# A macaron layer on one core: weight loads moved to GpSimd's queue, the bias added by a DMA

## The chip, the core and the metric

The kernel runs on one core of one Trainium2 chip. The metric is the device time of one launch in microseconds; the number to compare is the median of several runs.

## What is computed

The layer takes x of shape 2 x 1024 x 1024 in float32 and applies three residual steps: half a feed-forward step, attention, and the same half feed-forward step again, each behind a layernorm without weights:

```
x = x + 0.5 * ffn(layernorm(x))
x = x + attn(layernorm(x))
x = x + 0.5 * ffn(layernorm(x))

ffn(x)  = x @ base_w.T + base_b + 2.0 * sum over the top 2 of 8 experts of
          weight_e * (x @ lora_A[e].T) @ lora_B[e].T      # rank 16, gate: softmax of the top 2 of x @ gate_w.T
attn(x) = causal attention, 32 query heads, 8 key/value heads, width 32, rotary positions, then @ Wo
```

The bias base_b has 1024 entries. It is added with a factor of one half in both feed-forward steps.

## The kernel before

The 2048 rows of x are cut into 16 tiles of 128 rows. A tile goes through four stages, which the code calls a1 (first feed-forward step), a2 (products with Wq, Wk, Wv), c1 (product with Wo) and c2 (second feed-forward step); attention runs between a2 and c1 in units of one tile and one key/value head. In the order of instructions, dense stages of some tiles are cut into pieces and placed between the attention units of another.

Every float32 product is made from float16 parts: an operand is scaled and split into a high and a low half, and `dense` (L353 to L362) multiplies high by high, high by low and low by high (L358, L359, L360). So the beginning of the kernel has a preparation for each weight: it is loaded in float32, the sum of squares is taken (`pow2`, L165 to L188, with squares on ScalarE at L169, a small product on TensorE at L174 and a root on GpSimd at L177), and `split` (L190 to L195) writes the high half on ScalarE (L194) or, for every fourth block, on GpSimd (L192), and the low half on VectorE (L195). Base, gate and lora weights stay in SBUF (`wb`, `ag`, `lbh`, `lbl`). The five halves of Wq, Wk with Wv, and Wo are written back to HBM in their split form (`wstr`, L267) and streamed in for each tile by `prefetch` (L366 to L371) into three half buffers `ws` that are used in turn.

`layernorm` (L328 to L351) takes statistics on VectorE (L331, L333), a root on GpSimd (L335, L337), the normalised tile `xn` on ScalarE (L349), and has `Split.add` write its high (L310, ScalarE) and low half (L311, VectorE) to `hl`. A DMA transposition on SP's queue (L314) turns `hl` into `tt`, the left operand. `ffn` (L390 to L447) first multiplies `tt` with the gate and lora_A weights, then adds the bias `bb` to the tile with two GpSimd additions of 128 x 512 (L395), computes the expert weights (L398 to L420), makes the two base products (n = 0 and 1, L358 to L360, with the lora part at L440 to L442), and adds each to the tile on VectorE (L444).

Loads are issued by `load_x` (L124 to L127) for a tile of x and by `piece` (L143 to L163) for half a weight column block, 1 MB, in up to two DMAs; `stage` (L245) is `piece` for one of the streamed weights. Each takes the engine that issues the DMA. In the kernel before this is SP, except for Wk and Wv, which ScalarE's queue issues (L794, L795). `bb` is loaded by one DMA that repeats the bias on 128 partitions (L793), and is halved on ScalarE (L233, `prep_lora`). The beginning is written out in order at L770 to L831: loads, then a1 of tiles 0 to 2 in pieces, with the preparation between them.

The order of instructions on each engine is set by a scheduler that simulates a timeline, so an edit can move instructions that it doesn't name. `pin` (L117 to L120) keeps the DMAs of the beginning in the order of the program. A queue's DMAs are issued in order: one that waits holds up those behind it, and on GpSimd, whose DMAs stand in one order with its arithmetic, the arithmetic too.

Of the kernel before, what the change touches and what calls it, by code (L numbers as in the profile page):

```python
# [9 lines left out]
FP = mybir.dt.float32  # L10
# [3 lines left out]
ALU = mybir.AluOpType  # L14
AX = mybir.AxisListType

B, T, D = 2, 1024, 1024
NH, NKV, DH, GRP = 32, 8, 32, 4
E, R = 8, 16
P = 128  # L20
KB = D // P
# [18 lines left out]
def kernel(  # L40
# [16 lines left out]
    nc = tc.nc  # L57
# [3 lines left out]
    const = ctx.enter_context(tc.tile_pool(name="const", bufs=1))  # L61
    wres = ctx.enter_context(tc.tile_pool(name="wres", bufs=1))
    small = ctx.enter_context(tc.tile_pool(name="small", bufs=SB))
# [4 lines left out]
    dram = ctx.enter_context(tc.tile_pool(name="dram", bufs=1, space=bass.MemoryType.DRAM))  # L68
# [17 lines left out]
        out=cmask, in_=cmask, compare_op=ALU.is_ge, fill=-NEG, base=0,  # L86
# [14 lines left out]
    nc.gpsimd.memset(ones, 1.0)  # L101
    cosT = const.tile([P, TPB, DH // 2], FP)
    sinT = const.tile([P, TPB, DH], FP)
    bb = const.tile([P, D], FP)

    qst = [stat.tile([P, NH, P], HP, name=f"qst{j}") for j in range(2)]
    kst = stat.tile([P, NKV, P], HP)
# [9 lines left out]
    def pin(ins):  # L117

        if pinned[0]:
            tc.keep_in_program_order(ins)  # L120
# [3 lines left out]
    def load_x(t):  # L124
        xt = xp.tile([P, D], FP, name="xt")
        pin(nc.sync.dma_start(out=xt, in_=late["x"] if t == LATE and late else xf[bass.ts(t, P), :]))
        xts[t] = xt  # L127
# [15 lines left out]
    def piece(slot, srcs, h, eng):  # L143

        if slot < 0:
            st = wss[slot].rearrange("p a k n -> p (a k n)").bitcast(FP)
            st = st.rearrange("p (k n) -> p k n", n=512)
        elif slot >= 3:
            st = (qst + [kts[:, HK : 2 * HK]])[slot - 3]
            st = st.rearrange("p k h c -> p (k h c)" if slot == 5 else "p h c -> p (h c)")  # L150
            st = st.bitcast(FP).rearrange("p (k n) -> p k n", n=512)
        else:
            st = stg.tile([P, HK, 512], FP, name=f"st{slot}")
        c = 0
        for src in srcs:
            n = src.shape[1]
            ins = eng.dma_start(
                out=st[:, :, c : c + n],
                in_=src[h * (D // 2) : (h + 1) * (D // 2), :].rearrange("(k p) n -> p k n", p=P),
            )  # L160
            pin(ins)
            c += n
        return st  # L163
# [61 lines left out]
    def prep_lora(st):  # L225
        c = const.tile([P, 2], FP, name="sl")
        nc.vector.tensor_copy(c[:, 0:1], S["l",])
        nc.vector.scalar_tensor_tensor(c[:, 1:2], INV["b", 0], S["l",], S["b", 1], ALU.mult, ALU.mult)
        for n in range(2):
            h, s = bass.ts(n, 512), c[:, n : n + 1]  # L230
            nc.scalar.activation(lbh[:, h], st[:, h], AF.Copy, scale=s)
            nc.vector.scalar_tensor_tensor(lbl[:, h], st[:, h], s, lbh[:, h], ALU.mult, ALU.subtract)
        nc.scalar.mul(bb, bb, 0.5)  # L233

    KV = [wk_in, wv_in]
    CHUNKS = {
# [8 lines left out]
    def stage(ci, h, slot, eng):  # L245
        staged[ci, h] = piece(slot, CHUNKS[ci][0], h, eng)
# [4 lines left out]
    def prep_stream(ci, slots, after, keep):  # L251

        parts = CHUNKS[ci][1]
        sts = [staged.pop((ci, h)) for h in range(2)]
        sps = []
        for h in range(2):
            sps.append(wss[slots[h]] if slots[h] < 3 else kth)
            if h == 0:
                for name, c0, c1 in parts:
                    pow2([st[:, :, c0:c1] for st in sts], [sps[0][:, j, :, c0:c1] for j in range(2)], name)  # L260
                    yield
            sp = sps[h]
            for k in range(HK):
                for name, c0, c1 in parts:
                    split(sp[:, 0, k, c0:c1], sp[:, 1, k, c0:c1], sts[h][:, k, c0:c1], S[name], k)
                yield
            nc.scalar.dma_start(out=wstr[ci, h], in_=sp)  # L267
            if keep:
                stream.append((ci, sp))
            if after[h]:  # L270
                stage(*after[h], nc.sync)
            yield True

    def prep_rest():
# [115 lines left out]
    def ffn(xt, tt, done):  # L390
        psa = p_dense.tile([P, 512], FP, name="pd")
        yield from dense(psa[:, 0 : P + E], tt, lambda k: (ag[:, 0, k, :], ag[:, 1, k, :]))
        for n in range(2):
            c = bass.ts(n, 512)
            nc.gpsimd.tensor_tensor(xt[:, c], xt[:, c], bb[:, c], ALU.add)  # L395

        lg = small.tile([P, E], FP, name="lg")
        nc.scalar.activation(lg, psa[:, P : P + E], AF.Copy, scale=S["cg"])  # L398
        nv = small.tile([P, 1], FP, name="nv")
        nc.vector.tensor_reduce(nv, lg, AX.X, ALU.max, negate=True)  # L400
        ex = small.tile([P, E], FP, name="ex")
        nc.scalar.activation(ex, lg, AF.Exp, bias=nv)
        fe = lg.unsqueeze(1).to_broadcast([P, E, E])
        ee = lg.unsqueeze(2).to_broadcast([P, E, E])
        lw = small.tile([P, E, R], FP, name="lw", bufs=1)
        gt, eq = lw[:, :, 0:E], lw[:, :, E : 2 * E]
        nc.vector.tensor_tensor(gt, fe, ee, ALU.is_gt)
        nc.vector.tensor_tensor(eq, fe, ee, ALU.is_equal)
        nc.vector.tensor_tensor(eq, eq, tri, ALU.mult)
        nc.vector.tensor_tensor(gt, gt, eq, ALU.add)  # L410
        rk = small.tile([P, E], FP, name="rk")
        nc.vector.tensor_reduce(rk, gt, AX.X, ALU.add)
        nc.vector.scalar_tensor_tensor(ex, rk, 1.5, ex, ALU.is_lt, ALU.mult)
        sm = small.tile([P, 1], FP, name="sm")
        nc.vector.tensor_reduce(sm, ex, AX.X, ALU.add)
        nc.vector.reciprocal(sm, sm)
        nc.vector.tensor_scalar(ex, ex, sm, S["inva2"], ALU.mult, ALU.mult)
        nc.vector.tensor_tensor(
            lw, psa[:, 0:P].rearrange("p (e r) -> p e r", r=R),
            ex.unsqueeze(2).to_broadcast([P, E, R]), ALU.mult,  # L420
        )
        yield True
        psb = [None, None]
        lh = ll = None
        for n in range(2):
            ps = p_dense.tile([P, 512], FP, name="pd")
            psb[n] = ps
            yield from dense(
                ps, tt, lambda k: (wb[:, n, 0, k, :], wb[:, n, 1, k, :]), last=False
            )  # L430
            if n == 0:
                pst = p_s1.tile([P, GRP, P], FP, name="s1")[:, 0, :]
                nc.tensor.transpose(pst, lw.rearrange("p e r -> p (e r)"), ident)
                lh = small.tile([P, P], HP, name="lh", bufs=LB)
                ll = small.tile([P, P], HP, name="ll", bufs=LB)
                nc.scalar.copy(lh, pst)
                nc.vector.tensor_tensor(ll, pst, lh, ALU.subtract)
                yield
            c = bass.ts(n, 512)
            nc.tensor.matmul(ps, lhsT=lh, rhs=lbh[:, c], start=False, stop=False)  # L440
            nc.tensor.matmul(ps, lhsT=lh, rhs=lbl[:, c], start=False, stop=False)
            nc.tensor.matmul(ps, lhsT=ll, rhs=lbh[:, c], start=False, stop=True)  # L442
            yield
            nc.vector.scalar_tensor_tensor(xt[:, c], ps, S["uf", n], xt[:, c], ALU.mult, ALU.add)  # L444
            done(n)
            if n == 0:
                yield True  # L447

    def stage_a1(t):
        tt = layernorm(xts[t])  # L450
        yield

        def done(n):
            if n == 1:
                Ts["x2", t] = layernorm(xts[t])
                if t == LATE:
                    late["x"] = dram.tile([P, D], FP, name="xlate")
                    nc.sync.dma_start(out=late["x"], in_=xts.pop(t))

        yield from ffn(xts[t], tt, done)  # L460
        yield True
# [318 lines left out]
    gst = [agst[:, h] for h in range(2)]  # L780
    lst = xp.tile([P, D], FP, name="xt")
    pin(nc.sync.dma_start(out=lst, in_=lb_in))
    b0 = [piece(h - 2, [wb_in[:, 0:512]], h, nc.sync) for h in range(2)]
    load_x(1)
    a1 = [stage_a1(t) for t in range(3)]
    next(a1[0])
    prep_gate(gst)
    pow2([lst[:, bass.ts(h, 512)] for h in range(2)], [lbh[:, bass.ts(h, 512)] for h in range(2)], ("l",))
    b1 = [piece(3 + h, [wb_in[:, 512:1024]], h, nc.sync) for h in range(2)]
    prep_base(0, b0)  # L790
    load_x(2)
    next(a1[1])
    pin(nc.sync.dma_start(out=bb, in_=bias_in.partition_broadcast(P)))  # L793
    stage(2, 0, 0, nc.scalar)  # L794
    stage(2, 1, 1, nc.scalar)  # L795
    prep_base(1, b1)
    prep_lora(lst)
    stage(3, 0, 2, nc.sync)
    stage(3, 1, 5, nc.sync)
    stage(0, 0, 3, nc.sync)  # L800
    stage(0, 1, 4, nc.sync)
    next(a1[2])
    pin(nc.sync.dma_start(out=cosT, in_=cos_in.rearrange("(i p) d -> p i d", p=P)))
    pin(nc.sync.dma_start(out=sinT, in_=sin_in.rearrange("(i p) d -> p i d", p=P)))
# [235 lines left out]
```

## Time and profile before

| what | us |
|---|---|
| median of 3 runs | 1523.7 |
| lowest and highest | 1520.88, 1530.89 |
| profiled execution | 1528.72 |
| its span on the core | 1527.0 |
| TensorE busy in the span | 1404.1 |
| GpSimd busy in the span | 450.1 |
| GpSimd's bias additions (L395), 64 of them | 92.3 |

The profile is one execution, recorded by the hardware. PE is TensorE's matmul, PEld its weight load, DVE is VectorE, ACT ScalarE, POOL GpSimd, SP SyncE; SPq, ACTq and POOLq are the instruction queues of these engines where they issue DMAs. A line such as L395 is a line of the kernel before. Start times count from the start of the span. "Idle before, releaser" says how long an engine stood still ahead of an instruction and what ended it. DMA issues do not count as busy time of an engine. The granted clock is the share of full speed that TensorE was given.

### The profile page before, as it was taken

The page shows a single profiled execution, that of the slowest core. Times are in us where ns is not written, and L with a number is a line of the kernel's source. Part 1 is how long each engine was busy: PE and PEld are TensorE (multiplying, and loading weights), DVE is VectorE, ACT ScalarE, POOL GpSimd, SP SyncE. Part 2 cuts the span into 40 slices and gives each one's busy share as a digit, 9 for nine tenths or more (in the row PEclk, how much of TensorE's full clock was granted, in tenths as well). Part 3 has the DMA queues.
Part 4 walks back from the last instruction along what each step waited for, and adds up shares of the span by engine and source line. Part 5 has one row for each costly group of instructions (what it writes and reads, how often), then busy time and mean ns, then how long its engine had stood idle before and what let it go on. Part 6 is the DMA issues. An engine that isn't in the chain of part 4 may idle for free.

```text
span 1527.0 us, 35303 instructions
## 1 busy us (share of the span) xinstructions
PE 1404.1 (92%) x14548; PEld 783.4 (51%) x14548; DVE 1139.7 (75%) x2420; ACT 755.5 (49%) x1374; POOL 450.1 (29%) x665
## 2 busy tenths in 40 slices
PE   3686897989999999999999899999999999989998
PEld 2243444455555555555654445555555555556544
DVE  6877656686968879789764767886869788689753
ACT  7564334453545545456552434553545455556631
POOL 3443213432323233122121323332323232312231
PEclk9798999989999999999999999999999999999999
DMA  9957697658575581853646769857383853834651
GB/s 274 333 156 204 115 237 205 206 127 264 123 238 137 153 254 31 235 160 69 209 160 191 216 161 272 202 160 234 72 294 69 237 147 70 271 69 98 133 170 45
DMA packets 293075, 267.30 MB, mean 175 GB/s; under 512 B 258480, under 2 KB 261552, under 8 KB 272432
## 3 DMA queue, kind: packets, MB, share of 16 engines
q1 hardware_dynamic: 289360, 252.45, 60.5%
q10 hardware_dynamic: 3552, 12.58, 2.3%
q8 instruction: 114, 1.87, 0.5%
q14 instruction: 49, 0.40, 0.1%
HBM read 181.63 MB, written 20.45 MB: 132 GB/s over the span
## 4 chain that ended last, share of the span: by engine, by line
PE 65%; DVE 13%; DMA 13%; ACT 3%; issue 2%; POOL 1%; SPq 1%; DVEq 0%; ACTq 0%; POOLq 0%
PE pd L358 13%; PE pd L359 13%; PE pd L360 13%; PE av L657 10%; PE s L712 7%; PE s L573 6%; DMA ws<-wstr 6%; DMA qt<-qst 5%; DVE mx L590 3%; DVE pair L636 1%; DVE ws L195 1%; DMA tt<-hl 1%; DVE o L666 1%; ACT p L718 1%; DVE hl L311 1%
## 5 line engine op out<-in xcount | busy, mean ns | idle before, releaser
L718 ACT ACTIVATE p<-s,cs 128x512 f32<-128x512 f32 x576 | 382.3, 688 | 291.2 <-PE s L712 284.1
L590 DVE TENSOR_REDUCE mx<-s 128x4 f32<-128x512 f32 x480 | 313.6, 675 | 68.3 <-PE s L573 46.8
L358 PE MATMUL pd<-ws,tt 128*128 128x512 f16 x592 | 226.8, 383 | 20.9 <-DMA ws<-wstr 16.8
L636 DVE TENSOR_TENSOR pair<-p,p 128x512 f32<-128x512 f32 x256 | 185.6, 727 | 72.6 <-ACT p L718 34.8
L573 PE MATMUL s<-kts,qt 96*128 96x128 f16 x2304 | 217.0, 222 | 23.8 <-DMA qt<-qst 17.8
L359 PE MATMUL pd<-ws,tt 128*128 128x512 f16 x592 | 226.3, 382 | 0.0
L712 PE MATMUL s<-qt,kts 128*128 128x512 f16 x576 | 210.7, 386 | 16.4 <-DMA qt<-qst 11.6
L360 PE MATMUL pd<-ws,tt 128*128 128x512 f16 x592 | 225.4, 382 | 0.0
L573 PEld LDWEIGHTS <-qt 96*128 96x128 f16 x2304 | 165.5, 99 | 116.4 <-issue 30.4
L359 PEld LDWEIGHTS <-tt 128*128 128x128 f16 x1360 | 135.6, 100 | 141.9 <-issue 31.3
L358 PEld LDWEIGHTS <-tt 128*128 128x128 f16 x1360 | 135.6, 100 | 135.5 <-issue 16.7
L358 PE MATMUL pd<-wb,tt 128*128 128x512 f16 x512 | 199.0, 389 | 5.0 <-DVE xt L444 5.0
L360 PEld LDWEIGHTS <-tt 128*128 128x128 f16 x1360 | 135.3, 99 | 131.5 <-issue 10.2
L359 PE MATMUL pd<-wb,tt 128*128 128x512 f16 x512 | 198.0, 387 | 0.5 <-DVE wb L195 0.5
L360 PE MATMUL pd<-wb,tt 128*128 128x512 f16 x512 | 197.7, 386 | 0.0
L657 PE MATMUL av<-p,va 128*32 128x128 f32 x4608 | 166.8, 278 | 4.8 <-ACT o L664 2.5
L720 POOL TENSOR_SCALAR_AFFINE_SELECT p<-p 128x512 f32<-128x512 f32 x128 | 89.0, 698 | 274.7 <-ACT p L718 264.4
L673 POOL TENSOR_TENSOR tt<-o,tt 128x128 f16<-128x128 f32 x128 | 70.5, 551 | 279.6 <-ACT tt L672 279.3
L657 PEld LDWEIGHTS av<-p,va 128*32 128x32 f32 x4608 | 115.5, 110 | 68.3 <-issue 53.4
L666 DVE RECIPROCAL o<-o 128x128 f32<-128x128 f32 x128 | 120.6, 942 | 24.9 <-ACT o L664 24.9
L585 POOL TENSOR_SCALAR_AFFINE_SELECT sm<-sm 128x512 f32<-128x512 f32 x96 | 66.4, 692 | 203.9 <-ACT sm L584 202.1
L395 POOL TENSOR_TENSOR xt<-xt,bb 128x512 f32<-128x512 f32 x64 | 92.3, 1464 | 59.6 <-ACT xn L349 59.4
(177 smaller groups left out, 1808.2 us busy)
## 6 DMA issues: line engine op xcount, KB each, us to landing
ws<-wstr SPq DMA_DIRECT2D x148, 1024.0 KB, 5.9
wstr<-ws ACTq DMA_DIRECT2D x9, 1024.0 KB, 6.1
xt<-in_x_dram SPq DMA_DIRECT2D x16, 512.0 KB, 3.8
out_dram<-xt SPq DMA_DIRECT2D x15, 512.0 KB, 2.8
ws<-in_wb_dram SPq DMA_DIRECT2D x2, 1024.0 KB, 8.0
qst<-in_wb_dram SPq DMA_DIRECT2D x2, 1024.0 KB, 6.8
st<-in_wo_dram SPq DMA_DIRECT2D x2, 1024.0 KB, 10.0
kts<-in_wo_dram SPq DMA_DIRECT2D x2, 1024.0 KB, 12.0
```

Source lines behind the costliest of these rows:

```text
L358: nc.tensor.matmul(ps, lhsT=th, rhs=wh, start=(k == 0), stop=False)
L359: nc.tensor.matmul(ps, lhsT=th, rhs=wl, start=False, stop=False)
L360: nc.tensor.matmul(ps, lhsT=tl, rhs=wh, start=False, stop=(last and k == KB - 1))
L395: nc.gpsimd.tensor_tensor(xt[:, c], xt[:, c], bb[:, c], ALU.add)
L573: nc.tensor.matmul(ps[:, h, :], lhsT=q[0 : 3 * DH, h, :], rhs=KT[b0 + j][0 : 3 * DH, g, :], start=(not pem or h == 0), stop=not pem,)
L590: nc.vector.tensor_reduce(mx[:, odd, j, :], ps, AX.X, ALU.max)
L636: nc.vector.tensor_tensor(sums, us[i][1], us[i + 1][1], ALU.add)
L657: prev = nc.tensor.matmul(av[rows, i, :], lhsT=w, rhs=p32[:, h, :], start=(us[0][0] == 0 and n == 0), stop=(last and n == len(runs) - 1), ...
L666: nc.vector.reciprocal(rc, rc)
L712: ins = nc.tensor.matmul(ps.rearrange("p h k -> p (h k)"), lhsT=KT[b0 + j][:, g, :], rhs=q.rearrange("p h k -> p (h k)"), start=True, stop ...
L718: nc.scalar.activation(p32, ps, AF.Exp, scale=cs)
L720: nc.gpsimd.affine_select(out=p32, in_=p32, compare_op=ALU.is_ge, fill=0.0, base=0, pattern=[[0, GRP], [1, P]], channel_multiplier=-1,)
```

## The change

All float32 weight loads of the base, Wq, Wk, Wv and Wo move to GpSimd's queue; x, the gate and lora weights, the rotary tables and the transpositions stay on SP's. The bias is no longer kept on 128 partitions. It is loaded once as 128 x 8, halved on GpSimd, and stored to a 4 KB tensor `hb` in HBM. In each `ffn`, one DMA from GpSimd's queue reads `hb` for all 128 partitions and adds it to the tile of x in SBUF, in place of the two additions. The buffer `bb`, its load and its scaling on ScalarE are gone. The new small load and store stand behind the load of tile 1.

```diff
-    bb = const.tile([P, D], FP)
...
-        nc.scalar.mul(bb, bb, 0.5)
...
             if after[h]:
-                stage(*after[h], nc.sync)
+                stage(*after[h], nc.gpsimd)
...
-        for n in range(2):
-            c = bass.ts(n, 512)
-            nc.gpsimd.tensor_tensor(xt[:, c], xt[:, c], bb[:, c], ALU.add)
+        nc.gpsimd.dma_start(out=xt, in_=hb.partition_broadcast(P), accum_op=ALU.add)
...
-    b0 = [piece(h - 2, [wb_in[:, 0:512]], h, nc.sync) for h in range(2)]
+    b0 = [piece(h - 2, [wb_in[:, 0:512]], h, nc.gpsimd) for h in range(2)]
     load_x(1)
+    hs = small.tile([P, KB], FP, name="hs", bufs=1)
+    pin(nc.sync.dma_start(out=hs, in_=bias_in.rearrange("(p k) -> p k", k=KB)))
+    nc.gpsimd.tensor_scalar(hs, hs, 0.5, 0.0, ALU.mult, ALU.add)
+    hb = dram.tile([D], FP, name="hb")
+    nc.gpsimd.dma_start(out=hb.rearrange("(p k) -> p k", k=KB), in_=hs)
     a1 = [stage_a1(t) for t in range(3)]
...
-    b1 = [piece(3 + h, [wb_in[:, 512:1024]], h, nc.sync) for h in range(2)]
+    b1 = [piece(3 + h, [wb_in[:, 512:1024]], h, nc.gpsimd) for h in range(2)]
     prep_base(0, b0)
     load_x(2)
     next(a1[1])
-    pin(nc.sync.dma_start(out=bb, in_=bias_in.partition_broadcast(P)))
-    stage(2, 0, 0, nc.scalar)
-    stage(2, 1, 1, nc.scalar)
+    stage(2, 0, 0, nc.gpsimd)
+    stage(2, 1, 1, nc.gpsimd)
     prep_base(1, b1)
     prep_lora(lst)
-    stage(3, 0, 2, nc.sync)
-    stage(3, 1, 5, nc.sync)
-    stage(0, 0, 3, nc.sync)
-    stage(0, 1, 4, nc.sync)
+    stage(3, 0, 2, nc.gpsimd)
+    stage(3, 1, 5, nc.gpsimd)
+    stage(0, 0, 3, nc.gpsimd)
+    stage(0, 1, 4, nc.gpsimd)
```

## The prediction

> **What bounds the kernel now.** I read the page's busy shares first, then busy time by stage, then the chain and single rows where the change works.
>
> ```profile
> PE 1404.1 (92%) x14548; PEld 783.4 (51%) x14548; DVE 1139.7 (75%) x2420; ACT 755.5 (49%) x1374; POOL 450.1 (29%) x665
> ...
> L395 POOL TENSOR_TENSOR xt<-xt,bb 128x512 f32<-128x512 f32 x64 | 92.3, 1464 | 59.6 <-ACT xn L349 59.4
> ```
>
> TensorE is busy 92% of 1527.0 us, so 122.9 us of idle is all that a better order can win. GpSimd, whose adds (L395, 92.3 us) go away, is idle 71% of the time: its busy time as such is worth nothing. Busy time by stage (length, then busy time of PE, PEld, DVE, ACT, POOL, granted clock, DMA share, GB/s) shows where the idle lies:
>
> ```profile
> 0.00:60.00 60.00, 24.85 (x114) 13.79 (x114) 45.80 (x128) 42.74 (x69) 25.93 (x51) 0.85 0.95 276
> 60.00:160.00 100.00, 81.52 (x386) 37.96 (x387) 68.01 (x156) 47.94 (x73) 32.07 (x44) 0.90 0.75 222
> ...
> 600.00:700.00 100.00, 98.59 (x1241) 58.91 (x1240) 82.12 (x166) 57.24 (x101) 28.68 (x38) 1.00 0.58 161
> ...
> 900.00:1000.00 100.00, 94.48 (x947) 52.79 (x947) 76.80 (x171) 49.90 (x95) 36.42 (x57) 1.00 0.78 198
> ```
>
> The first 60 us hold 35.2 us of PE's idle, the next 100 us 18.5. From 160 us on, 1297.7 of 1367 us are busy: the remaining 69 us are scattered. So there are two questions: what the start gains, and what 32 new accumulating DMAs cost the full stages. The chain in the start (start, length, what):
>
> ```profile
> 19.70 9.36 DMA xt<-in_x_dram
> 29.07 0.69 DVE bst L331
> 29.77 1.12 DVE hl L311
> 30.92 5.57 DMA tt<-hl
> 36.54 0.30 PE pd L358
> ```
>
> Tile 2's x is issued at 19.70, behind two 1 MB pieces of the base weights on SP's queue, and takes 9.36 us where the median of all x loads is 3.5. VectorE waits for it in order, with tile 1's low half (L311) queued behind it, so tile 1's transposition starts at 30.92 and PE has its first product of tile 1 at 36.54.
>
> **The change, part by part.** The built order of the changed kernel gives what stands behind what on each queue.
>
> *Weights off SP's queue.* SP loses 12 loads, ACT 4; GpSimd gets these 16, one tiny scaling, one 4 KB store and 32 accumulates. Tile 2's x then has no weights ahead of it on its own queue. The Trainium skill, DMA: Bandwidth & Descriptors, section Issuing engines are not separate DMA queues, speaks against a gain: all queues share 16 DMA engines, and only issue time is saved. Read strictly, the 2.5 MB of this moment stay one lump: 9.36 us, gain 0. But its section Queues, rings and completion order has the engines go round between queues packet by packet; then the 0.5 MB need only about 1 MB moved, some 4 us, and the load ends near 24. The row (9.36 beside 3.5) can't choose between the two. It matters little: in the new DVE order tile 1's L311 stands ahead of tile 2's statistics, so tile 1 no longer waits for that load. I estimate its transposition at 26 to 27, so PE gets tile 1 at about 32: minus 4.5 us at this step.
>
> *Issuing on GpSimd.* No DMA is issued from GpSimd before. Bounds per issue: SP's plain loads take 0.43 us each at the start; the longest plain issue on ACT's queue is 2.64 us (wv, with a stall in it). The same page, Specifications, gives about 1 us to the first byte by software descriptors against 0.6 by hardware; this trace has only the hardware kind. I take 1.0 us. In the new order: after L187 (ends 14.56) come two base pieces, scaling, the 4 KB store; then L335 and L337 for tile 1 (before: 18.12 to 19.55); then four K/V pieces, and only then L177 of base half 0 (before: 20.09). At 1.0 us the first three end at 17.8 and hide under the wait for tile 1's statistics; the four K/V issues do not, so L177 comes at 23.6: plus 3.5 us. Next, two accumulates wait for the 4 KB store, which queues behind 2 MB on the same queue: about 25. After them stand GpSimd's own splits of base half 0 (L192, before: 21.57), now at about 28. VectorE's products (L195, before: done at 28.11) end near 30, so tile 0's first dense block ends near 32, not 30.0. But PE idled from 30.0 to 36.5 there, so this is covered as long as tile 1's products come at 36.5 or earlier; net of the first part, PE is then 2 to 4 us ahead. I count minus 3. Later issues (two wo, two wq pieces ahead of the K and V scales; two wq and two wo ahead of tile 0's second layernorm) are eight, and half of their 8 us, 4 us, is on the path: VectorE is full from 40 to 60 us, which hides the others. Without that cover it is 8.
>
> *The bias.* Removed: bb's 512 KB load (4.9 us to landing), L233 on ACT (1.05 us), 64 adds. In the start six adds run from 44.11 and collide with VectorE:
>
> ```profile
> 44.11 8.37 POOL L395 TENSOR_TENSOR xt<-xt,bb 128x512 f32<-128x512 f32 x6
> ```
> ```profile
> 31.47 0.21 DVE L407 TENSOR_TENSOR lw<-lg 128x64 f32<-128x64 f32 x1
> ...
> 46.46 1.21 DVE L407 TENSOR_TENSOR lw<-lg 128x64 f32<-128x64 f32 x1
> 47.59 1.30 DVE L408 TENSOR_TENSOR lw<-lg 128x64 f32<-128x64 f32 x1
> 48.81 0.74 DVE L444 SCALAR_TENSOR_TENSOR xt<-pd,uf,xt 128x512 f32<-128x512 f32 x1
> ```
> ```profile
> 44.24 0.61 PE L442 MATMUL pd<-lbh,ll 128*128 128x512 f16 x1 [1.69 <-DVE ll L437]
> 49.60 0.59 PE L358 MATMUL pd<-wb,tt 128*128 128x512 f16 x1 [4.76 <-DVE xt L444]
> ```
>
> The same tiny L407 takes 0.21 us alone and 1.21 beside the adds. Excess there: L311 0.9, L407 1.0, L408 1.1, L409 0.4, L410 0.5, together 3.9 us in a stage where VectorE is full. PE waits 4.76 us for L444. Without adds L444 can follow L442 at about 45; of the 4.76 us I count 3, since four other VectorE instructions stand in between, part of the 3.9 us. Together minus 5. In the full stages an add costs PE next to nothing: waits of PE on VectorE's mx and pair are 5.7 and 2.7 us over the whole run. I count minus 1.
>
> *32 accumulates.* Is each in time for L444? In the full stage xn of a tile ends at 659.5, L444 runs at 679.9: 20 us of cover; for the last tile 1501.9 to 1521.9. The nearest row, bb's load of the same shape, lands in 4.9 us; a queue full of weights may double it. So the wait is covered. What is not covered is the load on the engines. A plain 512 KB at the best 10 us window (410 GB/s) is 1.3 us of all 16 engines. By the skill's DMA page (Rules for kernel authors) an accumulate reads its destination too and writes it later: source, destination, write, 1.5 MB, 3.8 us as an estimate. Such DMAs are not in the trace; I take 2.6. 27 of them fall after 160 us, 70 us of DMA work, 5% on shares of 0.53 to 0.78. PE's waits for DMAs there:
>
> ```profile
> PE pd L358 <- DMA ws<-wstr: 16.8, 15, 2.2
> PE s L712 <- DMA qt<-qst: 11.6, 12, 2.1
> PE s L573 <- DMA qt<-qst: 9.3, 8, 2.4
> ```
>
> With tt's 3 these are 38 waits out of some 320 transfers, 12%. If each accumulate holds up one or two transfers by 2.6 us and 12% of these are waited for, it is 8 to 17 us; some of it lies in slack between the transfers, so I take 9. Ends: 0 (all slip into free slots) and 27 x 3.8 = 103 (every one on the path; excluded by the 12%), realistically 40.
>
> **Sum.** Against the profiled execution (1528.7 us, span 1527.0): start minus 3 plus 4 minus 5 is minus 4; full stages plus 9 minus 1. Plus 4. That execution lay 5 us above the median of 1523.7, so I put the same plus 4 on the median, 1528, and one more microsecond for the changed order in the stage from 60 to 160 us, whose waits for transpositions I can't place: 1529.
>
> **Rivals.**
>
> *Slower: accumulates hold up the streamed weights and q's transpositions.* One mechanism, in the stages with DMA shares over 0.7 (160 to 400, 800 to 1000 us). Three half buffers of weights are used in turn, so a load that lands late moves the next one. For: those 38 waits are short (2.4 us at most), so loads land close to their use and PE has little left over. Against: from 400 to 800 us PE is 97 to 99% busy at shares near 0.57. Price: 27 x 2.6 us x 0.35 on the path is 25 us, with the start's minus 4 and minus 1 1544; at 3.8 us each 1556. I give 1548. It decides, that is, passes 15 us, from about 0.27 of each delay on the path.
>
> *Slower: GpSimd's issue takes 2.6 us, not 1.* Then L177 of base half 0 comes at about 33.5 instead of 20.1, tile 0's first dense block ends 13 us later, of which 6.5 us of idle absorb half: plus 6.5; eight later issues at half: plus 10; minus 5 for the bias; plus 8 full stages: 1543. It decides from about 2 us an issue.
>
> *Faster: the start gains in full.* Tile 1's 4.5, PE's 4.8 before L444, 3.9 of collisions, and 18 matmuls that now run at half clock (0.43 us instead of 0.22) behind the waits of 49.6 and 61.2 us, 3.8: minus 17, with accumulates free: 1507. Against: VectorE is full from 40 to 60 us and bounds what the start can gain.
>
> **How the numbers follow.** Likeliest 0.40 (1529, own range 1513 to 1540); accumulates 0.30 (1548; nine in ten over 1%); issue 0.14 (1543; seven in ten over 1%); faster 0.16 (1507; some eight in ten over 1%). About 1%, 15 us, is what a measurement here tells from no change. Slower: 0.27 + 0.10 = 0.37, rounded up to 0.39 for the upper end of the likeliest; faster 0.13; same 0.48. The range leaves out half of the fast case and the end of the accumulates: 1508 to 1562.
>
> **What would show it.** Right: tile 1's tt starts near 27; the 4.76 us wait before L358 is gone and L407 takes 0.2 us throughout; no wait of L444 on a DMA; GpSimd's gaps of about 1 us per issue; PE's waits on ws and qt up from 37.7 us by 5 to 15. Wrong: L177 of base half 0 after 28 us (issue dearer), L444 waiting for the accumulate (cover gone), or PE's waits on ws and qt doubled.

## The result and the profile after

The changed kernel takes 1538.56 us (median of 7 runs, 1533.11 to 1549.86) against 1521.27 us before (7 runs, 1516.24 to 1530.89): ratio 1.0117, 95% interval 1.0089 to 1.0144. It is slower by 1.2%. Some executions, of e4, e5 and e8 below, run in a slower state at a lower granted clock; the ratios leave these out, the medians in us don't. The profiled execution took 1538.56 us with a span of 1536.9; that of before had a span of 1527.0. The granted clock over the whole span is 0.974 in both.

In the changed kernel lines up to L391 are one or two lower than before, later ones four: the first product of `dense` is L356 (L358 before), the transposition L312 (L314), the tile update L440 (L444), the accumulating DMA L391.

The page of the kernel after, its busy shares, the costliest VectorE group of attention, and the accumulating DMA (issues, KB each, median us to landing):

```profile
PE 1397.8 (91%) x14548; PEld 782.1 (51%) x14548; DVE 1111.7 (72%) x2420; ACT 753.4 (49%) x1373; POOL 397.8 (26%) x651
...
L632 DVE TENSOR_TENSOR pair<-p,p 128x512 f32<-128x512 f32 x256 | 177.1, 694 | 72.7 <-ACT p L714 30.7
...
xt<-hb POOLq DMA_DIRECT2D x32, 512.0 KB, 6.6
```

GpSimd and VectorE have less work, as the edit promised, and the kernel is slower all the same. Busy time by stage of the kernel after (columns as in the prediction) tells where to look:

```profile
0.00:60.00 60.00, 16.50 (x92) 10.75 (x93) 31.36 (x105) 35.06 (x53) 29.74 (x60) 0.97 0.90 232
60.00:160.00 100.00, 77.25 (x369) 36.45 (x366) 69.33 (x166) 54.59 (x88) 32.35 (x49) 0.90 0.77 228
600.00:700.00 100.00, 98.85 (x1187) 58.42 (x1186) 81.06 (x168) 52.95 (x96) 24.01 (x36) 1.00 0.63 167
```

PE has 16.50 us of work in the first 60 us where it had 24.85, and 77.25 in the next 100 where it had 81.52. From 600 to 700 us it is as busy as before (98.85 and 98.59). The times at which a tile's output is issued need no window, and they are used for every run below (the last tile goes out in two pieces; the table has the first):

| output of tile | before, us | after, us | lag |
|---|---|---|---|
| first | 276.42 | 282.28 | 5.9 |
| second | 346.51 | 360.48 | 14.0 |
| third | 428.95 | 442.96 | 14.0 |
| sixth | 726.02 | 744.07 | 18.1 |
| ninth | 1016.65 | 1034.42 | 17.8 |
| last | 1522.69 | 1532.38 | 9.7 |

The lag is 5.9 us at the first output, 14.0 at the second, grows by 4 us more, and shrinks towards the end. What is lost is lost early: before the first output and between the first and the second. PE's waits in the first 160 us (total, number, longest), first before, then after:

```profile
PE pd L358 <- DVE xt L444: 5.0, 2, 4.8
PE pd L358 <- DMA tt<-hl: 1.8, 2, 1.5
```
```profile
PE pd L356 <- DMA tt<-hl: 25.2, 2, 15.1
```

The 5.0 us of waiting for VectorE's tile update (L444, now L440) ahead of this product are gone, and 25.2 us of waiting for two transpositions have come: tile 0's and tile 2's. The chain of the first 100 us after, its DMAs:

```profile
3.36 10.90 DMA xt<-in_lb_dram
...
23.23 24.13 DMA xt<-in_x_dram
...
69.03 25.27 DMA tt<-hl
```

The lora_B load (issued at 3.36, buffer `xt`), the load of tile 2's x and the transposition of tile 2 took 10.90, 24.13 and 25.27 us; the first two took 5.4 and 9.36 before. ScalarE's queue of work shows what the first of them does, before and after (idle ahead and its releaser in brackets):

```profile
7.96 0.64 ACT L169 ACTIVATE ag<-ws 128x544 f16<-128x544 f32 x1
8.79 0.63 ACT L169 ACTIVATE lbh<-xt 128x512 f16<-128x512 f32 x1
...
10.03 1.22 ACT L349 ACTIVATE xn<-xt,nb,rs 128x1024 f32<-128x1024 f32 x1
```
```profile
12.04 0.66 ACT L168 ACTIVATE ag<-ws 128x544 f16<-128x544 f32 x1 [4.41 <-DMA ws<-in_gw_dram]
...
14.29 0.63 ACT L168 ACTIVATE lbh<-xt 128x512 f16<-128x512 f32 x1 [1.50 <-DMA xt<-in_lb_dram]
...
15.53 1.23 ACT L347 ACTIVATE xn<-xt,nb,rs 128x1024 f32<-128x1024 f32 x1
```

The square of the second gate half and of the lora weights stand ahead of tile 0's `xn`, and ScalarE works in order; the squares start 4 to 5.5 us later, each after a wait for its load, so `xn` starts at 15.53 instead of 10.03. The reason, which e5 and e6 below test, is the two base pieces, which are now issued on GpSimd's own queue at 2.71 us, ahead of or beside loads that were ahead of them on SP's. The bytes are the same. The DMA packets of the first 16 us, before and after:

```profile
DMA packets 3600, 4.23 MB, mean 264 GB/s; under 512 B 1168, under 2 KB 2192, under 8 KB 3600
```
```profile
DMA packets 3232, 4.23 MB, mean 264 GB/s; under 512 B 1312, under 2 KB 2336, under 8 KB 3232
```

4.23 MB in both: in these 16 us the second queue moved no more bytes, it changed which load is served first. The transposition of tile 0 is then issued at 21.62 (15.98 before) beside two more base pieces from GpSimd (19.07) and the K/V pieces behind them; SP's and PE's row after:

```profile
21.62 1.55 SPq L312 DMA_TRANSPOSE tt<-hl  x1
23.23 5.23 SPq L125 DMA_DIRECT2D xt<-in_x_dram  x1
29.79 58.77 SPq L312 DMA_TRANSPOSE tt<-hl  x2
```
```profile
40.40 0.29 PE L356 MATMUL pd<-ag,tt 128*128 128x136 f16 x1 [15.14 <-DMA tt<-hl]
```

PE's first product of tile 0 comes at 40.40; it came at 20.41 before.

### The profile page after: what moved, and what is told of

It reads as the page before. It is cut to its first block, busy times and chain, and to the rows that moved or that the text cites. A ratio compares the mean times of both kernels' runs of the same rounds, so it can differ in the third digit from the quotient of the medians.

```text
span 1536.9 us, 35336 instructions
## 1 busy us (share of the span) xinstructions
PE 1397.8 (91%) x14548; PEld 782.1 (51%) x14548; DVE 1111.7 (72%) x2420; ACT 753.4 (49%) x1373; POOL 397.8 (26%) x651
## 4 chain that ended last, share of the span: by engine, by line
PE 68%; DMA 15%; DVE 10%; ACT 3%; issue 2%; POOL 1%; SPq 1%; ACTq 0%; POOLq 0%; DVEq 0%
PE pd L356 13%; PE pd L357 13%; PE pd L358 13%; PE av L653 11%; PE s L708 7%; PE s L569 7%; DMA ws<-wstr 5%; DMA qt<-qst 4%; DMA tt<-hl 3%; DVE mx L586 2%; DMA xt<-in_x_dram 2%; ACT p L714 1%; DVE pair L632 1%; DVE ws L194 1%; DVE bst L329 1%
## 5 line engine op out<-in xcount | busy, mean ns | idle before, releaser
L356 PE MATMUL pd<-ws,tt 128*128 128x512 f16 x592 | 226.5, 383 | 18.0 <-DMA ws<-wstr 17.1
L569 PE MATMUL s<-kts,qt 96*128 96x128 f16 x2304 | 219.3, 222 | 25.2 <-DMA qt<-qst 21.6
L632 DVE TENSOR_TENSOR pair<-p,p 128x512 f32<-128x512 f32 x256 | 177.1, 694 | 72.7 <-ACT p L714 30.7
L358 PE MATMUL pd<-ws,tt 128*128 128x512 f16 x592 | 226.0, 382 | 0.0
L356 PEld LDWEIGHTS <-tt 128*128 128x128 f16 x1360 | 135.9, 100 | 160.8 <-DMA tt<-hl 32.2
L356 PE MATMUL pd<-wb,tt 128*128 128x512 f16 x512 | 197.2, 385 | 5.7 <-DVE lw L414 4.7
L358 PEld LDWEIGHTS <-tt 128*128 128x128 f16 x1360 | 135.5, 100 | 127.5 <-issue 5.6
L358 PE MATMUL pd<-wb,tt 128*128 128x512 f16 x512 | 196.6, 384 | 0.0
L669 POOL TENSOR_TENSOR tt<-o,tt 128x128 f16<-128x128 f32 x128 | 67.1, 524 | 311.0 <-ACT tt L668 310.9
L580 ACT COPY sm<-s 128x512 f32<-128x512 f32 x96 | 56.0, 583 | 78.1 <-PE s L569 70.9
```

Source lines behind the costliest of these rows:

```text
L356: nc.tensor.matmul(ps, lhsT=th, rhs=wh, start=(k == 0), stop=False)
L358: nc.tensor.matmul(ps, lhsT=tl, rhs=wh, start=False, stop=(last and k == KB - 1))
L569: nc.tensor.matmul(ps[:, h, :], lhsT=q[0 : 3 * DH, h, :], rhs=KT[b0 + j][0 : 3 * DH, g, :], start=(not pem or h == 0), stop=not pem,)
L632: nc.vector.tensor_tensor(sums, us[i][1], us[i + 1][1], ALU.add)
```

## The experiments

My theory after this reading: the loss is that of weight loads which no longer wait behind what is needed first, in the start only; the bias part is harmless or a gain. Rivals: GpSimd's queue itself (its issue, or its descriptors taking more of the engines), and the accumulates. All ratios are to the kernel before on the same chip; "on top" is the quotient of two such ratios.

| run | us | before | ratio | interval |
|---|---|---|---|---|
| e1 weights only | 1553.27 | 1522.43 | 1.0209 | 1.0169 to 1.0248 |
| e2 bias only | 1516.29 | 1522.43 | 0.9963 | 0.9939 to 0.9987 |
| e3 weights on ScalarE's queue | 1525.50 | 1522.43 | 1.0018 | 1.0000 to 1.0035 |
| e4 two accumulates | 1571.35 | 1522.43 | 1.0314 | 1.0268 to 1.0360 |
| e5 first pieces back on SP | 1532.84 | 1524.84 | 1.0033 | 1.0012 to 1.0053 |
| e6 only first pieces moved | 1535.12 | 1524.84 | 1.0067 | 1.0046 to 1.0088 |
| e7 bias, tile 2's x early | 1506.72 | 1524.84 | 0.9883 | 0.9844 to 0.9922 |
| e8 plain load behind accumulate | 1585.28 | 1524.84 | 1.0318 | 1.0269 to 1.0368 |
| e9 tile 2's x early alone | 1518.84 | 1523.80 | 0.9976 | 0.9961 to 0.9992 |
| e11 after, weights on ScalarE's queue | 1521.35 | 1523.80 | 0.9991 | 0.9968 to 1.0014 |
| e12 after, tile 0's xn first | 1543.25 | 1524.08 | 1.0125 | 1.0088 to 1.0163 |

**The two halves apart.** e1 is the kernel before with only its 16 weight loads on GpSimd's queue:

```diff
-    b0 = [piece(h - 2, [wb_in[:, 0:512]], h, nc.sync) for h in range(2)]
+    b0 = [piece(h - 2, [wb_in[:, 0:512]], h, nc.gpsimd) for h in range(2)]
...
-    stage(3, 0, 2, nc.sync)
+    stage(3, 0, 2, nc.gpsimd)
```

> The weights' loads on GpSimd's queue as in the changed kernel, the bias as before (bb on 128 partitions, two GpSimd additions). Theory Q (weights on a queue of their own take the DMA engines from SP's queue, so x and the transpositions land late: tile 0's transposition was awaited until 40.4 us, tile 2's x took 24.1 us): 8 to 14 us slower than before, ratio 1.005 to 1.009, and tile 2's x takes over 18 us here too. Theory A (the 32 accumulating DMAs cost the time, the queues nothing): ratio 0.998 to 1.002.

e2 has only the accumulating DMA, the weights stay where they were:

```diff
-        for n in range(2):
-            c = bass.ts(n, 512)
-            nc.gpsimd.tensor_tensor(xt[:, c], xt[:, c], bb[:, c], ALU.add)
+        nc.gpsimd.dma_start(out=xt, in_=hb.partition_broadcast(P), accum_op=ALU.add)
```

> The bias by the accumulating DMA as in the changed kernel, the weights on SP's and ScalarE's queues as before. Theory Q: the additions that go are worth about 4 us in the start, the accumulates cost up to as much in the stages behind it; ratio 0.996 to 1.003. Theory A: 1.007 to 1.012, and somewhere between 280 and 340 us a transposition of q that takes over 10 us beside two accumulates.

The weights alone cost 2.1%, more than either theory gave them; the bias alone gains 0.4%. One sign of the theory that the accumulates cost the time did come in e2 all the same: a transposition of q that PE waits for beside two accumulates (9.57 us at 304.55). I come back to it with the accumulates below. e1's first output is issued at 298.65, 22 us behind the kernel before, and the lag stays there to the end. Its chain in the start, DMAs and PE's first product:

```profile
2.81 11.60 DMA ws<-in_gw_dram
...
23.74 15.38 DMA tt<-hl
39.16 0.29 PE pd L358
...
74.55 27.77 DMA tt<-hl
```

This is the picture of the kernel after with no accumulate in it, so the accumulates do not cause what is lost in the first 160 us. With both halves the kernel is 0.9% faster than e1. That is more than the 0.4% that the bias edit is worth alone, but the intervals of the ratios do not tell the two apart.

**Which queue?** e3 is e1 with ScalarE's queue in GpSimd's place, e11 the kernel after with the same swap:

```diff
-    b0 = [piece(h - 2, [wb_in[:, 0:512]], h, nc.sync) for h in range(2)]
+    b0 = [piece(h - 2, [wb_in[:, 0:512]], h, nc.scalar) for h in range(2)]
```

> As the first, but the weights on ScalarE's queue, whose DMAs the hardware describes. If any second queue full of weights takes the engines from SP's: ratio 1.004 to 1.010 and tile 2's x over 18 us. If only GpSimd's queue does it (its descriptors, or its issues ahead of GpSimd's small steps): 0.998 to 1.003 and x under 12 us.

> The changed kernel with all its weight loads on ScalarE's queue in place of GpSimd's; the accumulating DMA stays on GpSimd's. If GpSimd's queue is at fault and the bias is worth its 0.4%: ratio 0.994 to 1.000. If a second queue full of weights is at fault whatever engine issues it: 1.006 to 1.012, near the changed kernel.

Both cost nothing or next to it (1.0018, 0.9991; on top of e2, which has e11's bias, e11 loses 0.3%, not clear of noise). But ScalarE's order of work changed with the edit. In e11 tile 0's `xn` stands ahead of the gate's squares, and its transposition is issued at 11.87, before the second base pieces (12.92) exist on any queue:

```profile
8.27 1.24 ACT L347 ACTIVATE xn<-xt,nb,rs 128x1024 f32<-128x1024 f32 x1 [2.03 <-DVE nb L342]
```

So these two runs do not show that the engine that issues is to blame. e10 asks that directly. It computes nothing of the layer: four pieces of 1 MB are issued from SP, ScalarE or GpSimd, and behind them on SP's queue either a transposition of 128 x 2048 or a 512 KB load of x, whose wait VectorE shows.

```diff
+        if eng is not None:
+            for i in range(4):
+                eng.dma_start(out=st[i], in_=src.rearrange("(k p) n -> p k n", p=P))
...
+            nc.sync.dma_start_transpose(out=tt, in_=hl)
...
+            nc.sync.dma_start(out=xt, in_=xf[0:P, :])
```

> None of the layer is computed: only the disputed wait is measured. Sixteen stretches, one after the other: four 1 MB weight pieces are issued from no queue, SP's, ScalarE's or GpSimd's, and some 3 us later a transposition of 128 x 2048 (or a 512 KB load of x) on SP's queue; each stretch waits for the last. If GpSimd's queue takes more than its share from SP's: transposition about 5 us alone, about 8 beside ScalarE's pieces, 14 or more beside GpSimd's. If only the bytes in flight count: the same within 2 us beside ScalarE's and GpSimd's. Behind the pieces on SP's own queue about 12 us in either case.

VectorE's row behind each, the wait in brackets. First the transposition, then the load, each alone, behind SP's pieces, beside ScalarE's, beside GpSimd's:

```profile
18.33 0.15 DVE L83 CAST g<-tt 128x1 f32<-128x1 f16 x1 [4.39 <-DMA tt<-hl]
...
34.65 0.15 DVE L83 CAST g<-tt 128x1 f32<-128x1 f16 x1 [13.70 <-DMA tt<-hl]
...
50.69 0.15 DVE L83 CAST g<-tt 128x1 f32<-128x1 f16 x1 [13.41 <-DMA tt<-hl]
50.88 0.74 DVE L89 TENSOR_TENSOR g<-g,st 128x1 f32<-128x1 f32 x4
...
67.68 0.15 DVE L83 CAST g<-tt 128x1 f32<-128x1 f16 x1 [14.37 <-DMA tt<-hl]
...
73.96 0.15 DVE L87 COPY g<-xt 128x1 f32<-128x1 f32 x1 [3.35 <-DMA xt<-in_x_dram]
...
89.70 0.15 DVE L87 COPY g<-xt 128x1 f32<-128x1 f32 x1 [12.94 <-DMA xt<-in_x_dram]
...
99.75 0.15 DVE L87 COPY g<-xt 128x1 f32<-128x1 f32 x1 [7.24 <-DMA xt<-in_x_dram]
...
102.81 0.16 DVE L89 TENSOR_TENSOR g<-g,st 128x1 f32<-128x1 f32 x1 [2.51 <-DMA st<-in_wb_dram]
...
114.71 0.15 DVE L87 COPY g<-xt 128x1 f32<-128x1 f32 x1 [7.20 <-DMA xt<-in_x_dram]
```

A repetition gave 4.3, 13.6, 13.6, 14.8 and 3.35, 12.9, 7.1, 7.2. The load is served in between when the pieces are on another queue (7.2 instead of 12.9). The transposition is not: 13.4 to 14.8 us whether the pieces are ahead of it on its own queue or on another. The four additions behind it (L89), one for each piece, show it again: behind the transposition they run without a wait, so all 4 MB had landed before it or with it; behind the load VectorE still waits 2.5 us each for the last pieces. And pieces from GpSimd delay it by at most 1.2 us more than ScalarE's. What the queue of its own was to give the transpositions, it does not give. This is one trace with two passes.

**The first two pieces.** e5 is the kernel after with these two back on SP's queue, behind the lora load; e6 is e2 with these two moved and nothing else.

```diff
-    b0 = [piece(h - 2, [wb_in[:, 0:512]], h, nc.gpsimd) for h in range(2)]
+    b0 = [piece(h - 2, [wb_in[:, 0:512]], h, nc.sync) for h in range(2)]
```

> The changed kernel with the first two base pieces back on SP's queue, behind the gate and lora loads; the other weights stay on GpSimd's. Theory Q1 (the first pieces share the engines with the gate and lora loads, which all wait for): the lora load lands in 5 to 6 us again, tile 0's transposition is issued near 16 us and the time falls by 6 to 10 us against the changed kernel: ratio to before 1.005 to 1.008. Theory Q2 (the loss comes from the transpositions beside later pieces): ratio 1.010 to 1.013, as the changed kernel.

> The bias by the accumulating DMA, and of the weights only the first two base pieces on GpSimd's queue, all others as before. Theory Q1: 6 to 10 us slower than the bias alone, ratio to before 1.001 to 1.003. Theory Q2: as the bias alone, 0.995 to 0.998.

Putting them back wins 0.8% on the kernel after; moving them alone loses 1.0% on e2. Both are more than I expected (6 to 10 us; they come to 13 and 16). ScalarE's rows, e5 and then e6:

```profile
10.89 1.23 ACT L347 ACTIVATE xn<-xt,nb,rs 128x1024 f32<-128x1024 f32 x1
```
```profile
12.74 0.66 ACT L168 ACTIVATE ag<-ws 128x544 f16<-128x544 f32 x1 [5.08 <-DMA ws<-in_gw_dram]
...
15.21 1.23 ACT L347 ACTIVATE xn<-xt,nb,rs 128x1024 f32<-128x1024 f32 x1
```

In e5 tile 0's `xn` is back at 10.89, in e6 it is at 15.21 as in the kernel after. e6's first output is issued at 277.57, e2's at 262.28. What is left in e5 is 0.7% over e2, and its chain names it, the transposition of tile 2 beside the later pieces from GpSimd:

```profile
56.53 26.39 DMA tt<-hl
```

**The order alone.** e12 is the kernel after, with ScalarE made to do tile 0's `xn` and high half before the gate's squares:

```diff
-    prep_gate(gst)
+    with tc.issue_after(late["copied", 0].ins):
+        prep_gate(gst)
```

> The changed kernel, all weights on GpSimd's queue, with one order changed: ScalarE makes tile 0's xn and its high half first, and only then the squares of the gate and lora weights, as the scheduler did by itself where the weights were on ScalarE's queue. GpSimd's order moves with it: the K/V pieces come ahead of the second base pieces. If the loss is that tile 0's transposition is issued late, behind 2 to 4 MB of pieces: it is issued near 12 us, lands by 20, and the time falls to a ratio of 1.001 to 1.007. If GpSimd's queue loses the time in another way: 1.010 to 1.014, as the changed kernel.

It does not help (1.0125), and I had expected it to. The transposition of tile 0 is issued at 11.24 and PE starts at 20.10, as early as in the kernel before. The loss has moved on. GpSimd's order changed too: its queue now issues K/V and two accumulates first and the second base pieces only at 26.80, beside tile 1's transposition (26.07), which takes 15.7 us. PE's rows:

```profile
20.10 0.27 PE L356 MATMUL pd<-ag,tt 128*128 128x136 f16 x1 [1.28 <-ACT ag L193]
...
41.86 0.30 PE L356 MATMUL pd<-ag,tt 128*128 128x136 f16 x1 [7.76 <-DMA tt<-hl]
```

Its first output is issued at 282.17, as late as after (282.28). An early start of tile 0 by itself is worth nothing here. e12 moved two orders at once, and so can't say which of two things took the gain: the next transposition meets the same pieces, and the weights behind it come later too (second base pieces at 26.80, the first Wo pieces at 60.65, where the kernel after has 19.07 and 49.33).

**The accumulates, doubled and with a load beside them.** e4 adds each half of the bias in two DMAs of a quarter, e8 lets a plain 512 KB load into a buffer that nothing reads follow each accumulate. Both are built on e2.

```diff
         nc.gpsimd.dma_start(out=xt, in_=hb.partition_broadcast(P), accum_op=ALU.add)
+        nc.gpsimd.dma_start(out=xt, in_=hb.partition_broadcast(P), accum_op=ALU.add)
```
```diff
+        nc.gpsimd.dma_start(out=junk, in_=hb.partition_broadcast(P))
```

> As the second, but each tile gets two accumulating DMAs of a quarter of the bias, one behind the other: 64 in place of 32. Theory A: twice the loss of the second, ratio 1.015 to 1.025. Theory Q: at most 6 us over the second, since outside the start transfers have slack; ratio 0.998 to 1.006.

> The bias by the accumulating DMA as in the second run, and behind each accumulate a plain DMA of the same 512 KB from GpSimd's queue into a buffer that nobody reads. It tells load on the engines from the wait of a second accumulate for the first. If the 3% of the doubled accumulates is load: ratio 1.01 to 1.02. If it is GpSimd standing still until the first accumulate has landed (6.6 us each): 0.998 to 1.003.

Both lose 3.1 to 3.2% to the kernel before, 3.5% on top of e2, more than any of my expectations. Their profiled executions ran at a lower granted clock (0.95) than the others, e8's in the start above all (0.78 in its first 160 us, 0.98 from 300 us on), so I take from them only where the lag arises. e8's is there at the first output (335.74, 59 us late) and changes little after that (59 to 67): 512 KB more for each tile cost no time that can be seen in the full stages and a great deal in the start, where a dozen of these loads come in the first 160 us. How much of the 59 us is the clock's is not shown. e4's lag goes on growing (25 us at the first output, 65 at the end); there the second accumulate has to wait for the first on GpSimd, with GpSimd's share of attention behind it, so e4 says little about the load of an accumulate.

**A version that beats both.** e9 is the kernel before with tile 2's x issued right behind tile 1's, e7 the same on e2:

```diff
     load_x(1)
+    load_x(2)
...
     prep_base(0, b0)
-    load_x(2)
```

> The bias by the accumulating DMA, weights as before, and tile 2's x issued right behind tile 1's, ahead of the second base pieces. If tile 2's x late behind the base pieces costs what the chain of before shows: the x lands by 16 us, tile 1's transposition starts by 27 us, and the time falls 3 to 6 us below the bias alone: ratio to before 0.992 to 0.995. If VectorE's full stretch from 40 to 60 us bounds the start: 0.996, no gain.

> The kernel before with one edit: tile 2's x is issued right behind tile 1's, ahead of the second base pieces. Bias and weights as before. If the two edits of the run that beat both kernels add up (bias alone 0.996, together 0.988): ratio 0.990 to 0.994. If the early x pays only without GpSimd's additions and bb's load: 0.997 to 1.001.

e9 gains 0.24% and e7 1.17%, 0.8% on top of e2. The product of e2's and e9's ratios is 0.9939, and e7's interval ends at 0.9922, so together they give more than the two gains added, if only just beyond the noise. VectorE in e2 and in e7, the statistics of tile 2:

```profile
33.37 1.29 DVE L329 BATCH_NORM_STATS2 bst<-xt 128x6 f32<-128x512 f32 x2 [4.21 <-DMA xt<-in_x_dram]
```
```profile
17.60 1.28 DVE L329 BATCH_NORM_STATS2 bst<-xt 128x6 f32<-128x512 f32 x2
```

They run at 17.60 without a wait instead of at 33.37 after 4.21 us of waiting. e7 (1506.72 us) is the best kernel of this study.

## Why the prediction was right and wrong

The number lies in the range (1508 to 1562), but slower by over 1% had a chance of 0.39 and no change one of 0.48. The likeliest value, 1529, was 9.6 us low, and of the 17.3 us by which the medians differ it had 5. That it came this near is in good part luck: the reason for it was not the one that worked. By its own steps:

**Weights off SP's queue, minus 4.5: wrong, and the step that failed.** I asked what leaves SP's queue and gets a place nearer the front there, and priced tile 2's x. I did not ask what the pieces overtake. The two first base pieces stood behind gate and lora loads on SP's queue and so came after them; on a queue of their own they are served beside them. `xn` of tile 0 slips from 10.03 to 15.53. e5 and e6 size this at 13 and 16 us. The Trainium skill, DMA: Bandwidth & Descriptors, section Queues, rings and completion order, which has the engines go round between queues, held the answer: I applied it to the load that gains by it (x) and not to those that lose. By the other section, Issuing engines are not separate DMA queues, no bytes are moved sooner, and the 4.23 MB of the first 16 us agree. The two together let expect that what one load wins another loses.

**Tile 1's transposition at 26 to 27, x2 landing near 24: wrong.** The transposition went out at 29.79 (30.92 before), and x2 landed at 47.4. x2 stood on SP's queue behind tile 0's transposition, whose tile PE could use only at 40.40. I had let transpositions and x share SP's queue as if it were free. e10 shows that a transposition gets no share beside other queues' pieces (13.4 to 14.8 us, and 13.7 behind them); going round between queues fits the plain load (7.2), not this. In the kernel after, tile 0's transposition made PE wait 15.14 us. I called tile 0's dense block covered because PE had 6.5 us of idle behind it; it ended at 48.9, not 32.

**Issuing on GpSimd at 1.0 us: right in size.** The rows after:

```profile
2.71 1.78 POOL L156 DMA_DIRECT2D ws<-in_wb_dram  x2
...
26.57 0.57 POOL L176 TENSOR_TENSOR ar<-ar,half 128x1 f32<-128x1 f32 x1
```

0.75 to 0.99 us each over all 16. The scale of base half 0 comes at 26.57 rather than 23.6 because the whole start is late, and stays under the 28 us that I had named as the sign of dearer issue. The rival with 2.6 us an issue (1543) is excluded.

**The bias, minus 5 and minus 1: right in sign, too small.** PE's wait for the tile update ahead of a base product (L358 on L444) fell from 5.3 us over the run to 0.2, and to 0.9 in e2, where only the bias changed. The tiny sums that took 1.21 us beside GpSimd's adds take 0.21 in both tiles (L403 after, at 46.11 and 57.97):

```profile
46.11 0.21 DVE L403 TENSOR_TENSOR lw<-lg 128x64 f32<-128x64 f32 x1
```

e2 measures the whole of it, accumulates included: 0.37%, 5.7 us. In attention the VectorE sums of pairs take 694 ns instead of 727, 8.5 us over 256 of them, and this follows the bias in every run: 727 to 730 ns with the additions (before, e1, e3, e9), 691 to 706 with the DMA. The adds had disturbed more than the start.

**32 accumulates, plus 9: right in size, in one place.** No wait of PE or VectorE for an accumulate is seen, as predicted. PE's waits on `ws` and `qt` over the whole run after:

```profile
PE s L569 <- DMA qt<-qst: 21.6, 10, 13.6
PE pd L356 <- DMA ws<-wstr: 17.1, 11, 2.7
PE s L708 <- DMA qt<-qst: 4.5, 6, 2.1
```

From 160 us on they sum to about 43 us against 37.7: plus 5, inside the 5 to 15 that I had named. But they are not the many short delays that I had priced: 13.6 us of them is one wait, for a transposition of q that was issued at 313 us, and from 400 us on the sum is 17.8 us in both. After, then e2, then before:

```profile
327.51 1.46 PE L569 MATMUL s<-kts,qt 96*128 96x128 f16 x12 [13.61 <-DMA qt<-qst]
```
```profile
283.42 10.40 SPq L312 DMA_TRANSPOSE tt<-hl  x1
...
294.53 10.24 SPq L549 DMA_TRANSPOSE qt<-qst  x3
```
```profile
302.14 3.06 SPq L314 DMA_TRANSPOSE tt<-hl  x1
```

Two accumulates (300.86, 304.91), weights and a transposition of `tt` were in flight around it. The other runs tell which of them it goes with. In all eight with one accumulate for each tile PE waits here once, 7.1 to 18.0 us; in the four with the additions its longest wait for q here is 2.4 to 6.2. (e4, with two accumulates, has none above 2.1.) In e2 no weights were moved, and the transposition of `tt` ahead of q's holds SP's queue for 10.40 us beside two accumulates (281.18, 285.21), where it takes 3.06 before. So the wait comes with the accumulates. An estimate of what one occupies: in e2 GpSimd's queue has little else, and its packets take 6.6% of 1512 us on 16 engines, 3.1 us for each accumulate; in e1 the same queue has only weights, 1.6 us for 512 KB. I had taken 2.6.

```profile
q0 software_dynamic: 4640, 16.78, 6.6%
```
```profile
q0 software_dynamic: 3840, 14.68, 2.9%
```

The rival that has accumulates hold up the streamed weights and q's transpositions everywhere (25 us, 1548) is excluded by e2, which is faster than before.

**The sum.** I had minus 4 in the start and plus 8 behind it. The lag of the three kernels behind the one before, in us, each from one profile:

| output of tile | e1, weights only | e2, bias only | after, both |
|---|---|---|---|
| first | 22.2 | -14.1 | 5.9 |
| second | 22.0 | -4.9 | 14.0 |
| eleventh | 24.2 | -9.8 | 15.9 |
| twelfth | 22.0 | -16.2 | 12.0 |
| last | 22.1 | -14.9 | 9.7 |

The weights cost some 20 us before the first output, without the bias edit (22.2) or on top of it (5.9 against -14.1), and at most 8 behind it; I had them at plus 1. By then the bias has won 14, where I had 5; what the other 9 are was not taken apart. Between the first and the second output the accumulates cost 8 to 9 us. Behind that the bias wins again, 4 to 6 us of it between the eleventh and the twelfth output in every run with the DMA (at most 2 in those with the additions); PE's idle there is 8.4 us before and 4.3 after. All in all the kernel after loses 4 us more behind the first output, where I had 8. So there are errors of 19 us one way and of 9 and 4 the other, which is why the number came out near. The medians differ by 17.3 us, the two profiled spans by 9.9; the before that was profiled lay above its median, so the last row is some 8 us too kind to all three.

**Slips in the working.** The 3.5 us given as the median of all x loads counts the stores of x too; the loads alone have 3.8. The higher price of the first rival adds up to 1555, not 1556, and it decides from 0.28 of each delay, not 0.27. None of them moves the result.

**What stays open.** With the first pieces back on SP the kernel still loses 0.7% to e2 (e5), with all pieces on ScalarE's queue 0.3%, not clear of noise (e11). e10 leaves GpSimd's queue at most 1.2 us per transposition to answer for, and no plain issue on it took over 0.99 us. What differs is when the later pieces go out. Both engines issue them in order with their own work: K/V and the first Wo pieces go out at 20.48 and 43.71 in e11, 23.48 and 49.33 after, 19.91 and 36.93 in e5. So neither early nor late alone tells these runs apart; which transposition the pieces meet may. That this timing is the whole cause of what is left was only argued; a kernel with GpSimd's queue and ScalarE's issue times was not tried.

## What to carry to other kernels

A queue is also an order: before loads are moved to a queue of their own, list what stood ahead of them and will now be served beside them, and which in-order engine waits for that first. Size such a move by the first thing that it delays in the start, not by the load that it frees. And try the halves of a change apart: here one half gained 0.4% and the other lost 2.1%. Where a change has two halves, the lag of each at the same few points tells more than the totals: here a loss of 22 us and a gain of 15 stood behind a lag of 10.

## What the runs showed of the hardware

- A transposition beside the pieces of another queue lands no sooner than behind them on its own: 13.4 to 14.8 us beside 4 MB of ScalarE's or GpSimd's pieces, 13.6 to 13.7 behind them on SP's queue, 4.3 to 4.4 alone; all 4 MB had landed when it did (e10). A plain 512 KB load gains from the other queue (7.1 to 7.2 us beside the pieces, 12.9 behind them, 3.35 alone).
- A DMA issue takes GpSimd 0.75 to 0.99 us (accumulates 0.885 to 1.219), the engine's arithmetic waiting behind it; SP's plain loads of the first 3.4 us took 0.40 to 0.51.
- An accumulating 512 KB DMA lands in 5.1 us at least, 6.6 in the median and 20.4 at most, the one plain load of the same shape in 4.9. By its queue's share it occupies the 16 engines for about 3.1 us (estimate from e2), a plain load of weights for 1.6 (from e1).
